# A convolution block in float32: splitting four of six Winograd products by column parity for seven blocks, with wide squares and a new planned order

## The chip, the cores and the metric

The kernel runs on one core of a Trainium2 chip. The core has a tensor engine (PE, with its weight loads shown apart as PEld), a vector engine (DVE), a scalar engine (ACT), a general engine (POOL) and a queue for transfers (SP). The metric is the device time of one execution in microseconds. Before the change it is 1743.63 us, the median of three runs (1743.13 to 1743.80).

## The reference, cut to what matters

The input x is 4 images of 128 channels by 128 by 128 pixels, all float32. Two layers follow each other, and each adds its result to its input.

```python
# layer 0
x = x + _L0_conv_ref(_gn(x), ...)     # twice the same block: on x and on x transposed, summed
# in the block, t = tokens x channels
t = _ln(t); y1 = _ln(t); t = t + silu(y1) @ W_out.T
y2 = _ln(t); wht = y2 @ W_whiten.T
k = square(relu(wht @ W_key.T)); kv = k @ W_value.T; r = sigmoid(wht @ W_recep.T)
t = t + r * kv
# layer 1
x = x + _L1_conv_ref(_gn(x), ...)     # 3x3 convolution of expert 0, bias, channel gate from the mean
```

`_gn` is a group norm over 32 groups of four channels, with statistics over a whole image. So layer 0 of an image can start only when all of its input has been read once, and layer 1 only when layer 0 of the whole image is done.

## The kernel before, in words

**Layer 0.** An image is 32 chunks of 512 pixels (`CH`), worked in 16 pairs; `layer0(g)` records the work of pair g (0 to 63 over the four images). A chunk is normalised (`st`, `rs`, `nb`, `t`), multiplied with the attention weights (`att`, line 954), normalised again and turned to channels, and then goes through four key products (`pk`, line 1033), a rectifier (`h`, line 1038), a square (line 1044 on ACT, line 1050 on DVE), four value products (`kv`, line 1071), one gate product (`pr`, line 1058), the gating `r` (line 1080, DVE) and the addition to x (line 1086, POOL). Line 1094 takes the statistics for the second group norm.

**Layer 1.** `conv(k, at)` records one block of 16 rows, eight per image, k from 0 to 31. It is a Winograd form along the rows: DVE makes six transforms `v0` to `v5` from the loaded rows `xc` (lines 1179 to 1193), six products `m0` to `m5` follow, and ACT and DVE combine them to four output rows (lines 1218 to 1239). A product is three matmuls on one PSUM bank, for the centre, left and right tap of a row (lines 1203 to 1205); the filters `uw` are reloaded per image and scaled (line 621), and four of them get a unit tap (line 627). `conv_setup(b, ...)` (lines 538 to 642) turns the image's statistics into the group norm and the gate: an aggregate (line 552), group means (`cpm`, 555), variances (`cpv`, 565), two small squeeze products (`cp`, 579, and `cpr`, 589), a tanh, and the scaled filters.

**Order.** No engine is programmed in the order of the text. Every operation is recorded with its engine, a cost and a priority (`op`), and `Plan.order` lists them once when the program is built: the earliest operation that can start wins, ties and near ties go by priority plus the number that `SHIFT` has for its name, and `ROOM` limits how many buffers of a kind are in use. So the convolution of image b is laid between the operations of layer 0 of image b+1, and that of the last image stands alone at the end. `FIRST_FILL` and the loop at the end of the kernel put filler products (`busy`, line 411) on PE where it has nothing else to do early in the run.

**What stands around the change.** Of the third image, blocks 17 to 23 are the last seven. In the trace, their products start at 1369, 1419, 1469, 1514, 1550, 1575 and 1593 us; the last value product of the fourth image starts at 1577.75 us. `SQUARES` says for each of the eight squares of a pair where it is done: the first row up to pair 16, the second from pair 17 (`SQUARES_AT`).

Of the kernel before, what the change touches and what calls it, by code (L numbers as in the profile page):

```python
# [23 lines left out]
    "R": -94.694, "Rc": 15.085, "Rm": -2.646, "S": 24.009, "T": -84.8, "Tz": -36.19, "W": -22.14,  # L24
    "ab": 37.315, "att": 1.644, "b": 31.731, "bn0": 11.794, "bn1": -17.35, "bn2": -15.592,
    "bx": 49.609, "c": 7.82, "cag": 6.719, "cav": -18.068, "cd": -103.804, "cp": -37.768,
    "cp1": -27.368, "cpm": -17.233, "cpr": -71.755, "cpv": -65.194, "cre": 48.407, "crt": -73.005,
    "csg": -26.086, "csp": -39.311, "cth": -29.247, "cve": 53.942, "e": 12.136, "e0": 14.7,
    "e1": -70.81, "e2": -55.971, "edge": 60.492, "fw": 14.887, "g": -16.106, "gag": -13.379,
    "gnb": -14.148, "gpm": -2.701, "gpv": -23.531, "grt": -1.635, "gsp": -6.989, "gve": -30.013,  # L30
    "hot": -13.329, "in": 26.361, "in0": 105.375, "kv": 3.816, "late": 12.753, "m0": 23.5,
    "m1": -101.213, "o": -54.585, "pk": 3.497, "pq": -18.954, "pr": 3.288, "q": -106.007,
    "raw": -61.508, "rc": -6.337, "re": -93.796, "silu": -97.676, "sq": -115.033, "sqd": -34.912,
    "t": -2.49, "tD": -49.255, "tR": 16.588, "tW": -20.948, "th": -60.823, "tt": 105.266,
    "u": 16.271, "us": -19.465, "ut": 67.807, "ut2": 9.337, "uw": -50.513, "v": 57.985, "w": 117.982,
    "w0": 44.736, "w1": -43.048, "w2": -6.943, "x": 70.181, "x1": -70.076, "xc": 6.78, "xd": 2.407,
    "xf": -58.371, "xo": -10.863, "xs": -54.606, "y": 24.867, "z": 15.121, "zD": 21.243,
    "zR": 18.813, "zW": -13.966,
}
SQUARES = (("DDAA", "DDAA"), ("AAAA", "AAAA"))  # L40
TAIL_BANKS = ("Bkv", "Btr", "Btr", "Bh", "Bconv", "Bh")
TAIL_HOMES = ("xc", "xc", "x", "x", "x", "xc", "xc", "x")
CONV_AT, CONV_STEP = 2.0, 2.0
LOOK = {'PE': 0.018, 'DVE': 0.087, 'ACT': 0.048, 'POOL': 0.004, 'SP': 0.048}
HASTE = 31.975
SQUARES_AT = 17
ROOM = dict(
    x=3, xd=2, xs=2, ut=3, t=7, z=2, y=2, zd=2, zc=2, td=2, tt=2, R=2, y2=2, h=6, r=2, xc=2, vt=3, v=4,
# [3 lines left out]
BACKLOG = 1.96  # L52
FIRST_U_ON_DVE = (2, 3)


XF_BUS, FIRST_XD, LATE_AT = 3.4, -25, -5
FILL_UNTIL, FILL_STEP = 330, 1.2
FIRST_FILL = {6: 3, 7: 2}
# [26 lines left out]
def S_ON(g):  # L85
    return "POOL" if T_BY_DMA(g) else "DVE"

# [155 lines left out]
def conv_preact_kernel(  # L243
# [42 lines left out]
        z=[P, SUB, C], y=[P, CH], y2=[P, CH], h=[P, CH], r=[P, CH],  # L286
        xc=[P, BLK_ROWS + 2, W], vt=[P, Q, W], v=[P, Q, W], yt=[P, Q, W], uw=[P, 3, P],
# [17 lines left out]
    def staged(name, n, src=None):  # L305
        t = sb.tile([P, n], F32, tag="h", name=name, bufs=ROOM["h"])
        if src is not None:
            nc.scalar.dma_start(t, src)
        return t
# [112 lines left out]
    READ, WRITE = (0, 0.85), (0, 0.4)  # L422

    def op(name, eng, cost, prio, emit, reads=(), writes=(), new=(), port=False, bus=0.0):
        return plan.op(name, eng, cost, prio + SHIFT.get(name, 0.0), emit, reads, writes, new, port, bus)
# [112 lines left out]
    def conv_setup(b, at):  # L538
# [90 lines left out]
        for i in (1, 2, 3, 4, 0, 5):  # L629
            t = ("uw", b, i)  # L630
            if b > 0:

                def fetch(i=i, t=t):
                    nc.sync.dma_start(make(t, "uw"), raw_u[i])

                op("uw", D, READ, at - 1, fetch, [(("raw", i), 0), (("ready", b - 1), 0)], [(t, 0)], [(t, "uw")], bus=0.65)
            op(
                "us", V, (0.52, 0.61), at, lambda i=i: scaled(i), [(c, 0), (t, 0)],
                [(t, 0), *([(("ready", b), 0)] if i == 5 else ())], (), True,
            )  # L640
            if i in TAP:
                op("ut2", V, (0.21, 0.29), at, lambda i=i: tapped(i), [(t, 0)], [(t, 0)], (), True)

# [92 lines left out]
    def layer0(g):  # L736
# [3 lines left out]
        if p * PAIR % PER == 0:  # L740
# [6 lines left out]
            for q in range(SUB):  # L747

                on_dve = k == 0 and q in FIRST_U_ON_DVE

                def lay(q=q, on_dve=on_dve):
                    rs, nb = gn0[b]
                    scale, bias = rs[:, q : q + 1], nb[:, q : q + 1]
                    if on_dve:
                        nc.vector.tensor_scalar(T[xd][:, q], T[xd][:, q], scale, bias, ALU.mult, ALU.add)
                    else:
                        nc.scalar.activation(T[xd][:, q], T[xd][:, q], AF.Identity, bias=bias, scale=scale)

                op(
                    "u", V if on_dve else A, (0.61, 0.7) if on_dve else (0.705, 0.82), g, lay, [(("gn0", b), 0), *((xd, a) for a in range(SUB))],  # L760
                    [(xd, ("u", q))],
                )
# [117 lines left out]
        for h in range(PAIR):  # L880
            r = (p * PAIR + h) % PER

            def turn(h=h, r=r):
# [5 lines left out]
                "ut", V, (0.61, 0.7), g, turn, [(xd, ("u", q)) for q in range(SUB)],  # L889
# [105 lines left out]
        for h in range(PAIR):  # L995
# [33 lines left out]
            for j in range(NH):  # L1029
                pk, hh = ("pk", g, h, j), ("h", g, h, j)  # L1030
# [6 lines left out]
                def relu(pk=pk, hh=hh, j=j):  # L1037
                    nc.scalar.activation(make(hh, "h"), T[pk], AF.Relu, bias=kbias[:, j : j + 1])  # L1038

                op("re", A, (0.572, 0.69), g, relu, [(pk, 0)], [(hh, 0)], [(hh, "h")])  # L1040
                if square_on(g, h, j) == "A":

                    def square(hh=hh):
                        nc.scalar.activation(T[hh], T[hh], AF.Square)  # L1044

                    op("sq", A, (0.52, 0.63), g, square, [(hh, 0)], [(hh, 0)])
                else:

                    def square(pk=pk, hh=hh, j=j):
                        nc.vector.scalar_tensor_tensor(  # L1050
                            T[hh], T[pk], kbias[:, j : j + 1], T[hh], ALU.add, ALU.mult
                        )

                    op("sqd", V, (0.605, 0.685), g, square, [(hh, 0), (pk, 0)], [(hh, 0)])
# [11 lines left out]
            for j in range(NH):  # L1066

                def value(j=j, kv=kv, h=h):
                    if j == 0:
                        make(kv, "Bkv")  # L1070
                    nc.tensor.matmul(T[kv], wv[:, j, :], T["h", g, h, j], start=(j == 0), stop=(j == NH - 1))  # L1071
# [3 lines left out]
                    [(("wv", "c"), 0), (("h", g, h, j), 0), *([(kv, j - 1)] if j else ())],  # L1075
# [32 lines left out]
    def conv(k, at):  # L1108
# [29 lines left out]

        def units(s):
# [8 lines left out]
        def put(n, tag):  # L1148
            if tag == "v" and ending:
                t = sb.tile([P, CH], F32, tag="h", name=n, bufs=ROOM["h"])  # L1150
                T[name_of(n)] = t.rearrange("p (q w) -> p q w", w=W)
                return T[name_of(n)]
            return make(name_of(n), tag)

        def do(name, eng, cost, fn, reads=(), writes=(), new=(), port=False):
            new = [(t, "h" if tag == "v" and ending else tag) for t, tag in new]
# [3 lines left out]
        TWO = (0.605, 0.685)  # L1160

        def inner(name, tag, fn, rows_in=(), tiles_in=(), extra=(), cost=TWO, inplace=False):
# [7 lines left out]
            else:  # L1170
                reads += [(("turned", k - 1, half), v) for v in HALVES[half]]
            do(
                "v" if tag == "v" else "pq", V, cost, fn, reads + ([(t, 0)] if inplace else []), writes,
                () if inplace else [(t, tag)], True,
# [3 lines left out]

        inner("p", "vt", lambda: stt(put("p", "vt"), rows(2), -4.0, rows(4), ALU.mult, ALU.add), (2, 4))
        inner("q", "vt", lambda: stt(put("q", "vt"), rows(1), -4.0, rows(3), ALU.mult, ALU.add), (1, 3))  # L1180
        inner(
            "v1", "v", lambda: stt(put("v1", "v"), get("p"), gn["mg6"], get("q"), ALU.add, ALU.add), (),  # L1182
            ("p", "q"), [(("gn1", b), 0)], (0.655, 0.73),
        )
        inner("v2", "v", lambda: tt(put("v2", "v"), get("p"), get("q"), ALU.subtract), (), ("p", "q"))
        inner("p2", "vt", lambda: tt(put("p2", "vt"), rows(4), rows(2), ALU.subtract), (2, 4))
        inner("q2", "vt", lambda: tt(put("q2", "vt"), rows(3), rows(1), ALU.subtract), (1, 3))
        inner("v3", "v", lambda: stt(put("v3", "v"), get("q2"), 2.0, get("p2"), ALU.mult, ALU.add), (), ("p2", "q2"))
        inner("v4", "v", lambda: stt(put("v4", "v"), get("q2"), -2.0, get("p2"), ALU.mult, ALU.add), (), ("p2", "q2"))
        inner("v0a", "v", lambda: tt(put("v0", "v"), rows(0), rows(2), ALU.subtract), (0, 2))  # L1190
        inner("v0b", "v", lambda: stt(get("v0"), get("v0"), 4.0, get("p2"), ALU.mult, ALU.add), (), ("p2",), inplace=True)
        inner("v5a", "v", lambda: tt(put("v5", "v"), rows(5), rows(3), ALU.subtract), (5, 3))
        inner("v5b", "v", lambda: stt(get("v5"), get("q2"), -4.0, get("v5"), ALU.mult, ALU.add), (), ("q2",), inplace=True)

        def product(i):
            tag = TAIL_BANKS[i] if ending else "Bconv"
            m, v = name_of(f"m{i}"), name_of(f"v{i}")

# [9 lines left out]

        def t0(n):
            return (name_of(n), 0)  # L1210

        def outer(name, fn, reads, writes, new=(), port=False):
# [5 lines left out]
            lambda: nc.scalar.activation(put("e1", "yt"), get("m1"), AF.Identity, bias=gn["beta"]),  # L1218
            [t0("m1"), (("gn1", b), 0)], [t0("e1")], [(name_of("e1"), "yt")],
        )  # L1220
        product(2)
# [4 lines left out]
            "e", A, (0.572, 0.69), lambda: nc.scalar.copy(put("e3", "yt"), get("m3")), [t0("m3")],  # L1226
            [t0("e3")], [(name_of("e3"), "yt")],
        )
        product(4)
# [91 lines left out]
```

## Time and profile before

| | |
|---|---|
| median of the runs | 1743.63 us |
| profiled execution | 1742.63 us |
| its span, first to last instruction | 1740.9 us |
| mean granted clock of PE | 0.997 of full |
| PE, DVE, ACT, POOL busy | 97%, 82%, 74%, 68% |
| HBM traffic over the span | 203 GB/s |
| key and value products on PE | 480.9 and 525.8 us busy |
| the three lines of the convolution products on PE | 197.7, 195.4 and 194.9 us busy |

A group line of the profile reads: line, engine, operation, tile written and tiles read, shape, count, then busy time in all and the mean of one in ns, then the idle time of that engine just before, and what ended it. A timeline line reads: start and length in us, engine, line, operation, tiles, shape, number of instructions merged, and in brackets the idle time before. A float32 matmul stands in the trace as two records. The ends of matmuls are modelled, so the pace of PE is read from starts.

### The profile page before, as it was taken

How to read it: one execution, taken by the hardware profiler on the slowest of the kernel's cores; microseconds unless marked ns; L12 is line 12 of the kernel's file. 1: busy time of each engine (PE TensorE's matmuls, PEld its weight loads, DVE VectorE, ACT ScalarE, POOL GpSimd, SP SyncE). 2: the span in 40 equal slices, each digit the busy share in tenths (PEclk: the TensorE clock that was granted, in tenths of full speed). 3: DMA queues.
4: the chain of work that ended last, by engine and by line, in shares of the span. 5: the costliest groups of instructions: out<-in, count | busy, mean ns of one | idle time of the engine just before them, and what ended most of it. 6: DMA issues, size and time to landing. Idle time of an engine off the chain costs nothing.

```text
span 1740.9 us, 18709 instructions
## 1 busy us (share of the span) xinstructions
PE 1690.7 (97%) x4872; PEld 815.7 (47%) x4872; DVE 1424.9 (82%) x2619; ACT 1293.8 (74%) x2656; POOL 1184.0 (68%) x1085
## 2 busy tenths in 40 slices
PE   5899999999999999999999999999999999999999
PEld 2444544444444445444445445454544444444443
DVE  5898888788889967798998887888897766448986
ACT  1999998898988887889889877998887875440000
POOL 1778887788987885879777886988878773310000
PEclk9999999999999999999999999999999999999999
DMA  9366675466577777578778877577776565215321
GB/s 326 91 213 202 193 219 194 145 206 230 153 250 246 252 230 236 199 232 247 250 245 245 254 238 240 178 218 236 241 254 199 183 204 176 101 75 224 154 98 73
DMA packets 140170, 354.66 MB, mean 204 GB/s; under 512 B 19079, under 2 KB 78750, under 8 KB 122782
## 3 DMA queue, kind: packets, MB, share of 16 engines
q1 hardware_dynamic: 139472, 352.99, 63.1%
q8 instruction: 39, 0.64, 0.2%
q14 instruction: 69, 0.57, 0.1%
q10 hardware_dynamic: 590, 0.46, 0.1%
HBM read 230.31 MB, written 123.07 MB: 203 GB/s over the span
## 4 chain that ended last, share of the span: by engine, by line
PE 71%; ACT 10%; POOL 8%; DVE 7%; DMA 2%; issue 2%; SPq 0%; ACTq 0%; DVEq 0%; POOLq 0%
PE kv L1071 19%; PE pk L1033 18%; PE m L1203 7%; PE m L1204 7%; PE m L1205 7%; PE att L954 5%; PE pr L1058 5%; ACT t L839 2%; ACT h L1038 2%; POOL rs L820 2%; ACT z L839 2%; DVE st L770 1%; ACT h L1044 1%; POOL x L1026 1%; POOL t L908 1%
## 5 line engine op out<-in xcount | busy, mean ns | idle before, releaser
L1071 PE MATMUL kv<-h,wv 128*128 128x512 f32 x1024 | 525.8, 598 | 4.6 <-DVE r L1080 2.6
L1033 PE MATMUL pk<-y,wk_s 128*128 128x512 f32 x1024 | 480.9, 595 | 4.7 <-ACT h L1038 3.1
L1038 ACT ACTIVATE h<-pk,kbias 128x512 f32<-128x512 f32 x512 | 336.1, 682 | 90.9 <-PE pk L1033 88.3
L1033 PEld LDWEIGHTS pk<-y,wk_s 128*128 128x128 f32 x1024 | 190.0, 190 | 239.3 <-issue 178.1
L1071 PEld LDWEIGHTS kv<-h,wv 128*128 128x128 f32 x1024 | 183.0, 190 | 205.3 <-issue 164.1
L1044 ACT ACTIVATE h<-h 128x512 f32<-128x512 f32 x444 | 267.5, 629 | 2.6
L1086 POOL TENSOR_TENSOR x<-x,r 128x512 f32<-128x512 f32 x128 | 169.8, 1327 | 132.0 <-DVE r L1080 128.5
L820 POOL TENSOR_TENSOR rs<-rs,nhalf 128x8 f32<-128x8 f32 (+1 forms) x134 | 227.2, 1700 | 47.3 <-ACT rs L817 45.1
L839 ACT ACTIVATE z<-t,nb,rs 128x128 f32<-128x128 f32 x512 | 208.7, 489 | 21.8 <-POOL nb L825 20.9
L839 ACT ACTIVATE t<-ut,nb,rs 128x128 f32<-128x128 f32 x512 | 209.7, 488 | 8.5 <-POOL nb L825 4.8
L908 POOL TENSOR_TENSOR t<-t,g 128x512 f32<-128x512 f32 x124 | 161.2, 1301 | 68.0 <-ACT t L839 67.6
L770 DVE BATCH_NORM_STATS2 st<-t 128x6 f32<-128x256 f32 x512 | 187.1, 410 | 22.9 <-POOL t L911 22.7
L1203 PE MATMUL m<-v,uw 128*128 128x512 f32 x384 | 197.7, 596 | 3.9 <-DVE v L1182 3.9
L1204 PE MATMUL m<-v,uw 128*128 128x508 f32 x384 | 195.4, 590 | 0.0
L1205 PE MATMUL m<-v,uw 128*128 128x508 f32 x384 | 194.9, 589 | 0.0
L1015 POOL TENSOR_TENSOR y<-tt,R 128x512 f32<-128x512 f32 x96 | 130.9, 1367 | 59.8 <-PE pk L1033 46.9
L1026 POOL TENSOR_TENSOR x<-tt,x 128x512 f32<-128x512 f32 x124 | 162.5, 1324 | 3.9 <-DMA tt<-ts 3.7
L911 POOL TENSOR_TENSOR t<-t,b 128x512 f32<-128x512 f32 x124 | 162.7, 1319 | 2.6
L954 PEld LDWEIGHTS att<-wo,y 128*128 128x128 f32 x1024 | 130.9, 192 | 51.7 <-issue 33.1
L1063 ACT ACTIVATE r<-pr,rbias 128x512 f32<-128x512 f32 x128 | 87.1, 681 | 72.6 <-PE pr L1058 36.2
L1058 PE MATMUL pr<-y,wr_s 128*128 128x512 f32 x256 | 132.3, 600 | 3.9 <-ACT h L1038 3.0
L954 PE MATMUL att<-wo,y 128*128 128x128 f32 x1024 | 132.8, 276 | 0.4 <-ACT y L947 0.3
(160 smaller groups left out, 2278.6 us busy)
## 6 DMA issues: line engine op xcount, KB each, us to landing
xd<-in_x SPq DMA_DIRECT2D x128, 256.0 KB
x<-in_x SPq DMA_DIRECT2D x32, 1024.0 KB
xo<-x SPq DMA_DIRECT2D x32, 1024.0 KB
R<-rd SPq DMA_DIRECT2D x63, 512.0 KB
ts<-td SPq DMA_DIRECT2D x248, 128.0 KB
tt<-ts SPq DMA_DIRECT2D x62, 512.0 KB
out<-xc SPq DMA_DIRECT2D x31, 1024.0 KB
xc<-xo SPq DMA_DIRECT2D x24, 1152.0 KB
```

The lines of the kernel that those rows point to most:

```text
L770: nc.vector.bn_stats(st[:, i : i + 2, :].rearrange("p n f -> p (n f)"), two)
L820: nc.gpsimd.tensor_tensor(T[rs][:, part], T[rs][:, part], nhalf[:, :k], ALU.pow)
L839: nc.scalar.activation(dst[:, s, :], src[:, s, :], AF.Identity, bias=nb[:, i : i + 1], scale=rs[:, i : i + 1])
L954: nc.tensor.matmul(pa[:, ts(m, P)], T[y][:, ts(m, P)], wo2, start=True, stop=True)
L1033: nc.tensor.matmul(make(pk, "Bh"), wk_s[:, ts(j, P)], T[y2], start=True, stop=True)
L1038: nc.scalar.activation(make(hh, "h"), T[pk], AF.Relu, bias=kbias[:, j : j + 1])
L1044: nc.scalar.activation(T[hh], T[hh], AF.Square)
L1058: nc.tensor.matmul(make(pr, "Bh"), wr_s, T[y2], start=True, stop=True)
L1071: nc.tensor.matmul(T[kv], wv[:, j, :], T["h", g, h, j], start=(j == 0), stop=(j == NH - 1))
L1203: nc.tensor.matmul(pc, u[:, 1], vv, start=True, stop=False)
L1204: nc.tensor.matmul(pc[:, :, 1:W], u[:, 0], vv[:, :, 0 : W - 1], start=False, stop=False)
L1205: nc.tensor.matmul(pc[:, :, 0 : W - 1], u[:, 2], vv[:, :, 1:W], start=False, stop=True)
```

## The change

Five things are done together.

- For blocks 17 to 23 (`PARITY`) products 0, 1, 3 and 5 are split by the parity of the pixel's column. The transform v is laid down with the even columns in one half of the tile and the odd ones in the other. With filter taps u0, u1, u2, an even output needs u1 of the even column, u0 of the odd one before and u2 of the odd one beside it; and u1 of even plus u2 of odd is u1 of (even + odd) plus (u2 - u1) of odd. So one matmul of u1 with the sum of the halves (`su`, `cm`) serves both parities, and each parity has two matmuls of its own, with the differences of the filters (`ud`). The shared product is added by DVE (`cs`). Each of these matmuls has 256 columns or 252.
- Squares of two neighbours are done by ACT as one instruction of 1024 elements (`W`); the rectified tiles become double tiles (`h`, three instead of six). Up to pair 16 three instead of four squares of a pair stay on DVE.
- `FIRST_FILL` loses an entry: two instead of five early filler products on raw input.
- `zd` and `td` go from two buffers to one; the transforms of the last image take `t` tiles instead of `h` tiles.
- All the numbers of the planner (`SHIFT`, `LOOK`, `HASTE`, `BACKLOG`, `XF_BUS`) are new, so the order of the whole program is.

```diff
-SQUARES = (("DDAA", "DDAA"), ("AAAA", "AAAA"))
+SQUARES = (("DAWW", "DDWW"), ("WWWW", "WWWW"))
+SUM_BANK = "Btr"
-LOOK = {'PE': 0.018, 'DVE': 0.087, 'ACT': 0.048, 'POOL': 0.004, 'SP': 0.048}
-HASTE = 31.975
+LOOK = {'PE': 0, 'DVE': 0.079, 'ACT': 0.059, 'POOL': 0.002, 'SP': 0.194}
+HASTE = 63.69
 ROOM = dict(
-    x=3, xd=2, xs=2, ut=3, t=7, z=2, y=2, zd=2, zc=2, td=2, tt=2, R=2, y2=2, h=6, ...
+    s=2, ud=4,
+    x=3, xd=2, xs=2, ut=3, t=7, z=2, y=2, zd=1, zc=2, td=1, tt=2, R=2, y2=2, h=3, ...
-FIRST_FILL = {6: 3, 7: 2}
+FIRST_FILL = {7: 2}
+def PARITY(k):
+    return (0, 1, 3, 5) if 17 <= k < 24 else ()
...
+                    nc.vector.tensor_tensor(make(ud, "ud"), u[:, 0::2], u[:, 1:2].to_broadcast([P, 2, P]), ALU.subtract)
+                op("ud", V, (0.335, 0.42), at, beside, [(t, 0)], [(ud, 0)], [(ud, "ud")], True)
...
+                elif how == "W" and not first:
+                    def square(hh=hh):
+                        x = T[hh].rearrange("p a b -> p (a b)")
+                        nc.scalar.activation(x, x, AF.Square)
...
+            if tag == "v" and int(n[1]) in halves:
+                whole = T[name_of(n)].rearrange("p q w -> p (q w)")
+                T[name_of(n)] = whole.rearrange("p (e q k) -> p q k e", e=2, q=Q)
...
+                def both(i=i, su=su):
+                    x = flat_halves(i)
+                    dst = make(su, "s").rearrange("p (q k) -> p q k", q=Q)
+                    nc.vector.tensor_tensor(dst, x[:, 0], x[:, 1], ALU.add)
...
+                def parts():
+                    bank = make(m, tag)
+                    pc = bank.rearrange("p (e q k) -> p e q k", e=2, q=Q)
+                    T[m] = bank.rearrange("p (e q k) -> p q k e", e=2, q=Q)
+                    u, d, x = T["uw", b, i], T[ud], flat_halves(i)
+                    nc.tensor.matmul(pc[:, 0], d[:, 1], x[:, 1], start=True, stop=False)
+                    nc.tensor.matmul(pc[:, 0, :, 1:], u[:, 0], x[:, 1, :, : W // 2 - 1], start=False, stop=True)
+                    nc.tensor.matmul(pc[:, 1], d[:, 0], x[:, 0], start=True, stop=False)
+                    nc.tensor.matmul(pc[:, 1, :, : W // 2 - 1], u[:, 2], x[:, 0, :, 1:], start=False, stop=True)
+
+                def shared():
+                    nc.tensor.matmul(make(mm, SUM_BANK)[:, : CH // 2], T["uw", b, i][:, 1], T[su], start=True, stop=True)
...
+            def add():
+                t = by_parity(get(n))
+                row = T[name_of(f"mm{i}")][:, : CH // 2].rearrange("p (q k o) -> p q k o", q=Q, o=1)
+                tt(t, row.to_broadcast([P, Q, W // 2, 2]), t, ALU.add)
```

## The prediction

> **What bounds the kernel now.** I read the busy shares of the page first, then the table by stages, then the timeline of the tensor engine (PE) at the three places where it is not full.
>
> ```profile
> span 1740.9 us, 18709 instructions
> PE 1690.7 (97%) x4872; PEld 815.7 (47%) x4872; DVE 1424.9 (82%) x2619; ACT 1293.8 (74%) x2656; POOL 1184.0 (68%) x1085
> ...
> 300.00:400.00 100.00, 94.76 (x309) 47.79 (x308) 82.56 (x162) 89.64 (x186) 80.42 (x76) 0.98 0.56 177
> 1200.00:1300.00 100.00, 99.85 (x277) 47.53 (x276) 90.98 (x159) 85.44 (x177) 87.03 (x75) 1.00 0.77 240
> 1300.00:1400.00 100.00, 100.00 (x275) 47.24 (x274) 77.47 (x143) 78.58 (x162) 78.86 (x69) 1.00 0.58 192
> 1400.00:1500.00 100.00, 100.00 (x281) 47.87 (x280) 64.79 (x107) 61.95 (x118) 50.65 (x41) 1.00 0.52 170
> 1500.00:1600.00 100.00, 99.53 (x251) 45.06 (x250) 60.56 (x107) 35.77 (x63) 18.49 (x15) 1.00 0.37 141
> ```
>
> In the stage rows the columns after the length are PE, weight loads, DVE, ACT, POOL. From 1200 to 1600, where the convolution of the third image runs beside layer 0 of the fourth, PE is full and DVE is idle for 9.0+22.5+35.2+39.4 = 106 us. There PE work is time. Busy is no proof of pace, so I take starts:
>
> ```profile
> 1500.16 1.95 PE L954 MATMUL att<-wo,y 128*128 128x128 f32 x16
> 1501.95 1.02 PE L1071 MATMUL kv<-h,wv 128*128 128x512 f32 x2
> 1502.81 5.31 PE L1033 MATMUL pk<-y,wk_s 128*128 128x512 f32 x12
> 1507.96 0.59 PE L1071 MATMUL kv<-h,wv 128*128 128x512 f32 x1
> ```
>
> Twelve 512-column records take 1507.96-1502.81 = 5.15 us, 429 ns each; sixteen 128-column ones 1.79 us, 112 ns each. A float32 product is two records.
>
> The places where PE is not full: the start, about 300 to 330, and the close, between the last value product of the fourth image and its first convolution product.
>
> ```profile
> 29.49 7.20 PE L411 MATMUL fill<-xf,gmat 128*128 128x512 f32 x10
> 36.53 0.95 PE L498 MATMUL pm<-mv,gturn 128*128 128x1 f32 x8
> ...
> 31.04 1.02 DVE L493 BATCH_NORM_AGGREGATE mv<-st 128x2 f32<-128x192 f32 x1
> 37.74 0.17 DVE L509 COPY mg<-pm 128x5 f32<-128x5 f32 x1 [5.67 <-PE pm L500]
> ...
> 303.05 1.05 PE L498 MATMUL pm<-mv,gturn 128*128 128x1 f32 x8 [1.73 <-ACT h L1038]
> ...
> 1577.75 1.02 PE L1071 MATMUL kv<-h,wv 128*128 128x512 f32 x2
> 1578.61 1.02 PE L1203 MATMUL m<-v,uw 128*128 128x512 f32 x2
> 1581.17 1.02 PE L1203 MATMUL m<-v,uw 128*128 128x512 f32 x2
> ...
> 1612.37 2.07 PE L1203 MATMUL m<-v,uw 128*128 128x512 f32 x2 [3.42 <-DVE v L1182]
> ```
>
> The statistics of the first image are whole at 32.06, but the group means stand behind filler products until 36.53. One convolution product (three matmuls) costs 1581.17-1578.61 = 2.56 us. From the last value product's end (1578.61) to the first product of the fourth image's convolution 33.8 us pass; eleven products (28.2 us) cover most of it, and 3.42 us stay idle. The last 48 products and the last store take 1740.9-1612.4 = 128.5 us.
>
> **The change part by part.** *Split products.* Each of 28 products becomes four matmuls over half the columns and one shared one. A 256-column record, on the line between the two rows above, is 112+(429-112)/3 = 218 ns, a 252-column one 214 ns. Product: (3x218+2x214)x2 = 2.16 us against 2.56; 28x0.40 = **11.2 us less PE work**. Bounds: 11.8 if it is half of 429 exactly, 0 if weight loads surface (rival). The weight loads of the 128-column rows hide at 112 ns a pair, so I keep 11.2.
>
> The Trainium skill ("TensorE: Matmul & The Clock Gate", LDWEIGHTS, and Part 3, The mechanism) says that a load takes its columns over 1.2 GHz, about 107 ns, and that loads run beside matmuls in flight only when they use other rows of the array. With ten records a product instead of six that would be an estimated 0.43 us more and would eat the whole saving. The 112 ns pairs above, each with its load, speak against it here.
>
> *Vector work for it.* 28 sums of halves (256 elements; nearest row, the 256-element statistics, 410 ns, issued every 0.33), 28 additions of the shared product (nearest row, the 512-element additions from PSUM, 681 ns, issued every 0.60), 4 differences of filters (0.4): 9.2+16.8+1.6 = 28 us of DVE, in a stage with 106 us idle. Hidden, price 0. Ops that write or read the halves interleaved keep 0.60 by the row of the statistics, which hop 512 bytes between neighbours and take 410 ns for 256 elements against 674 for 512 contiguous ones; the far end is 1.2 us, about 12 ops x 7 blocks x 0.6 = 50 us more. 28+50 = 78 is still under 106; only the close would feel it (below). The skill ("SBUF — State Buffer", the note on cachelines in Door 1) warns that each step past a 16-byte line costs; by it the far end would hold, and the statistics row does not show such a cost for reads. No row shows it for writes.
>
> *Squares.* 444 narrow squares on ACT (629 ns, issued every 0.52) and 68 on DVE become 17, 222 wide ones and 51. A wide one lies between 0.52 (nothing for width) and 1.04 (twice); I take 0.95. ACT -11 us, DVE -10 us over the run; neither bounds. A wide square makes the first value product of a pair wait for the second activation, about 0.6 us, while PE takes other chunks' products; without that cover 256 pairs x 0.6. h has three double tiles for six single ones, the same bytes. Price 0, from -3 to +3.
>
> *Rooms.* zd and td drop to one buffer: a pair's two transposes on DVE (and all behind them) now wait for the four stores of the pair before on SP's queue, not of two before. Pairs are about 25 us apart (the value products of pairs 48 and 52 start at 1181.4 and 1278.7), a store is 128 KB. Price 0; without cover a few us each. POOL keeps its work; SP gets no new transfer, but the places of many move.
>
> *Fewer early products.* Five fillers on raw input become two. They start at 29.45 at half clock (0.85 a record), four records end at 32.9: the means start right behind the statistics, not at 36.5. But the clock that became full at 34.9 will not have by then: the earlier small products show 1.71/8 = 0.21 us a record at half clock against 0.11, so means and variances lose 2 us of the 3.6. **-1.8**, between -3.6 and 0 (the 15 fillers that follow run cold and push the first transposition).
>
> *New order.* Everything is planned again. The built order has the second image's means at 10.9 pairs of value products instead of 11.4, so half a pair (10 us) more work behind them to cover the change of images. Idle there: 1.73 and 0.94 us before products, smaller ones, and 3.4 us at clock 0.5 from 304.5, some 7 us. I take **-2.5**; bounds 0 and -7. Elsewhere PE waits little and I take 0.
>
> *The close.* In the new order only two ordinary, three split and two shared products follow the last value product: 2x2.56+3x1.73+2x0.43 = 11.2 us instead of 28.2. So PE does 28.2-11.2-11.2 = **5.8 us more before** that point, which then stands at 1578.6+5.8-1.8-2.5 = 1580.1. After it, by the rows of before and the new order: means product behind shared, ordinary, shared, split (5.2), variances behind an ordinary one (8.0), squeeze product behind split, shared, split (12.2); rectify 1.0 (1591.95 to 1592.98), second product 0.4, tanh 0.7, the first vectors of the new block and the row 1.9: 16.2. Then six scalings 0.57 each, an output sum, four taps, the border and the first transform, 6.0: **22.2 us**, against 33.8. PE idles 10 us of it, and as in before (clock 0.5 for 3.4 us from 1611.8) restarts cold: 0 to 1.7 more than before, 0.5 taken. Bounds for the close: 18 (no queue on DVE) and 36.8, when nothing overlaps: 12.4 PE + 19.8 DVE (the 44 instructions that the new order has there, at their spacing in before) + 4.6 of round trips. It is nearest to the low end since DVE's queue there loses most of two blocks.
>
> **Sum.** First product of the fourth image at 1580.1+22.2 = 1602.3, 10.1 earlier; +0.5 cold: -9.6 us. The profiled execution took 1742.63 (span 1740.9 and 1.7 around it), 1.0 under the median of 1743.63. 1742.63-9.6 = 1733.0, and on the median's scale **1734.0**.
>
> **Rivals.**
> - *More comes in:* close at 18, change of images -7, start -3.6: 1734.0-4.2-4.5-1.8 = **1723.5**. For it: a whole new order; against: each at its bound.
> - *Interleaved vectors cost double and the early gains fail:* in the close seven such ops add 4.2; start and change of images give nothing (+4.3): **1742.5**, no change.
> - *Weight loads surface:* nothing saved on PE; the last value product comes 28.2-12.9-4.3 = 11.0 later than before, close 23.5: 1613.1, with 0.5 cold 1.2 later: **1744.8**. Against it: the 112 ns pairs.
> - *Slower, the close serialises:* DVE is in order, and block 23's sums stand between the setup steps, each behind a PE product. At 36.8 the first product comes at 1616.9, 4.5 late, +0.5: **1748.6**. The gain is gone from 31.8 us on, and it is slower by 0.2% from 35.3 on. For it: before took 33.8; against it: in before DVE had two blocks to finish there.
>
> **How the numbers follow.** About 0.2% (3.5 us) is what a measurement of this kernel can tell from no change. Forecast 0.54, more 0.21, no change 0.10, loads 0.07, slower 0.08. Faster: the first two and a little of the third, 0.76; same: the rest of the third and half of the loads' case, with the noise of both, 0.14; slower 0.10. The range takes in most of the first rival and reaches to the second: 1726 to 1743. The forecast's own range is 1729 to 1739.
>
> **What would show it.** Records of 256 columns about 218 ns apart; means at 33 us, not 36.5; PE still full from 1200 on, with DVE some 28 us busier; the last value product near 1580 and the first product of block 24 some 22 us after it, behind about 10 us of idle PE and a cold clock. Wrong would be: starts of the split records near 270 ns, DVE full beside an idle PE before 1580, or a close above 32 us.

## The result, and the profile after

The changed kernel takes 1750.80 us (median of 20 runs, 1743.03 to 1757.16); the kernel before, run beside it, takes 1742.85 (1739.00 to 1748.51). The ratio is 1.0045, with a 95% interval of 1.0034 to 1.0057: **slower by 0.45%, 8 us**, where 9.6 us less were forecast. The profiled execution of the changed kernel took 1748.30 us, 2.5 under its median.

The busy shares of its page, and the shares of the engines in the chain of work that ended last:

```profile
span 1746.6 us, 18860 instructions
PE 1679.6 (96%) x4978; PEld 834.5 (48%) x4978; DVE 1439.8 (82%) x2662; ACT 1282.7 (73%) x2451; POOL 1190.5 (68%) x1085
...
PE 53%; POOL 17%; DVE 12%; ACT 8%; DMA 5%; issue 3%; SPq 1%; ACTq 0%; DVEq 0%; POOLq 0%
```

The same stage rows as before (after the length: PE, weight loads, DVE, ACT, POOL, then the granted clock):

```profile
300.00:400.00 100.00, 98.84 (x320) 49.00 (x319) 78.60 (x158) 96.96 (x191) 82.85 (x80) 1.00 0.58 191
1200.00:1300.00 100.00, 98.48 (x283) 47.45 (x282) 86.23 (x167) 83.90 (x163) 82.00 (x73) 1.00 0.73 235
1300.00:1400.00 100.00, 97.80 (x303) 52.83 (x302) 80.24 (x134) 63.05 (x109) 60.65 (x49) 1.00 0.53 176
1400.00:1500.00 100.00, 96.74 (x317) 54.04 (x316) 81.10 (x130) 66.00 (x114) 57.28 (x49) 1.00 0.52 171
1500.00:1600.00 100.00, 99.05 (x288) 52.97 (x286) 67.54 (x105) 46.92 (x64) 28.85 (x21) 1.00 0.32 112
```

PE is busy for 11 us less, and the span is 5.7 us longer. From 1200 to 1500, where PE stood at 99.85 to 100, it is now at 96.7 to 98.5. DVE between 1300 and 1600 went from 202.8 to 228.9 us. In the chain PE's share is 53%, where it was 71%, and POOL (17% after 8%) and DVE (12% after 7%) have most of what PE lost: the chain runs through waits more often.

The PE timeline at the three places that the prediction spoke of: the start, a split product, the close.

```profile
29.67 3.76 PE L422 MATMUL fill<-xf,gmat 128*128 128x512 f32 x4
33.22 1.71 PE L511 MATMUL pm<-mv,gturn 128*128 128x1 f32 x8
...
1593.91 1.02 PE L1116 MATMUL kv<-h,wv 128*128 128x512 f32 x2
...
1597.33 0.59 PE L1302 MATMUL mm<-s,uw 128*128 128x256 f32 x2
1597.76 0.59 PE L1296 MATMUL m<-v,ud 128*128 128x256 f32 x2
1598.19 0.59 PE L1297 MATMUL m<-v,uw 128*128 128x252 f32 x2
...
1608.93 0.48 PE L602 MATMUL cpr<-s,a 16*128 16x128 f32 x2 [1.62 <-DVE a L596]
...
1617.16 2.07 PE L1312 MATMUL m<-v,uw 128*128 128x512 f32 x2 [7.63 <-DVE v L1253]
```

The means start at 33.22 (36.53 before). Two 256-column records take 0.43 us, 215 ns each (216 in the median of the stage). The last value product starts at 1593.91 and ends about 1594.8; block 24 starts 22.4 us later. All this is as forecast. But the last value product was to stand near 1580, and it stands 16 us later than before: part of that is convolution work moved ahead of it, and the rest is waits. The following rows of waits on PE between 1300 and 1600 (engine, what waited, for what: us in all, times, longest) name the longest:

```profile
PE kv L1116 <- DVE r L1125: 1.8, 2, 1.3
PE mm L1302 <- DVE e L1325: 1.7, 1, 1.7
PE mm L1302 <- DVE s L1281: 1.3, 2, 0.9
```

The idle time of PE can be summed from the starts of its matmuls: what a start-to-start distance has over its columns/1.2 + 2.7 ns (429 ns for 512 columns, by the rows of before) is idle or a cold clock. By pairs of layer 0:

| idle and cold, us | before | after | after's order, whole products |
|---|---|---|---|
| to pair 3 | 42.0 | 41.0 | 42.4 |
| pairs 4 to 15 | 17.4 | 14.8 | 14.9 |
| pairs 16 to 47 | 16.4 | 24.2 | 25.7 |
| pairs 48 to 63 | 4.5 | 13.9 | 6.8 |
| close | 6.6 | 13.1 | 11.0 |

PE's own work fell by 11.7 us through the split and 2.6 through three fewer fillers; idle rose by 20.1. Two places gave it back: pairs 16 to 47, where no product is split, and pairs 48 to 63, where they are. (The 6.5 us more in the close stood in the forecast, as some 10 us of idle PE there.) Each column is one execution; the second and third took 2.5 us less and 3.0 us more than their medians, so a few us between these two columns mean little. The rise in pairs 16 to 47 is no accident of one execution: in four more traces of the new order (whole products with two buffers, plain transforms, and both kernels without sums) it is 7 to 11 us.

### The profile page after: what moved, and what is told of

The parts are those of the page before. It is cut to its first block, busy times and chain, and to the rows that moved or that the text cites. A ratio compares the mean times of both kernels' runs of the same rounds, so it can differ in the third digit from the quotient of the medians.

```text
span 1746.6 us, 18860 instructions
## 1 busy us (share of the span) xinstructions
PE 1679.6 (96%) x4978; PEld 834.5 (48%) x4978; DVE 1439.8 (82%) x2662; ACT 1282.7 (73%) x2451; POOL 1190.5 (68%) x1085
## 4 chain that ended last, share of the span: by engine, by line
PE 53%; POOL 17%; DVE 12%; ACT 8%; DMA 5%; issue 3%; SPq 1%; ACTq 0%; DVEq 0%; POOLq 0%
PE kv L1116 14%; PE pk L1058 13%; PE m L1312 5%; PE m L1313 5%; PE m L1314 5%; POOL rs L845 4%; PE pr L1103 4%; PE att L979 3%; DMA xs<-in_x 2%; POOL t L933 2%; POOL x L1131 2%; POOL t L936 2%; POOL four L816 2%; ACT t L864 2%; ACT z L864 2%
## 5 line engine op out<-in xcount | busy, mean ns | idle before, releaser
L1058 PE MATMUL pk<-y,wk_s 128*128 128x512 f32 x1024 | 494.6, 596 | 9.0 <-ACT h L1064 3.4
L1064 ACT ACTIVATE h<-pk,kbias 128x512 f32<-128x512 f32 x512 | 340.3, 680 | 111.7 <-PE pk L1058 72.9
L845 POOL TENSOR_TENSOR rs<-rs,nhalf 128x8 f32<-128x8 f32 (+1 forms) x134 | 234.2, 1753 | 38.3 <-ACT rs L842 38.2
L1083 ACT ACTIVATE h<-h 128x1024 f32<-128x1024 f32 x222 | 234.1, 1055 | 2.2
L1312 PE MATMUL m<-v,uw 128*128 128x512 f32 x328 | 169.1, 597 | 10.1 <-DVE v L1253 8.8
L1313 PE MATMUL m<-v,uw 128*128 128x508 f32 x328 | 167.3, 592 | 0.0
L1314 PE MATMUL m<-v,uw 128*128 128x508 f32 x328 | 166.9, 591 | 0.0
L816 POOL TENSOR_TENSOR four<-four,nhalf 128x8 f32<-128x8 f32 x63 | 110.5, 1756 | 21.4 <-ACT four L812 21.3
```

Source lines behind the costliest of these rows:

```text
L845: nc.gpsimd.tensor_tensor(T[rs][:, part], T[rs][:, part], nhalf[:, :k], ALU.pow)
L1058: nc.tensor.matmul(make(pk, "Bh"), wk_s[:, ts(j, P)], T[y2], start=True, stop=True)
L1064: nc.scalar.activation(dst[:, j % 2], T[pk], AF.Relu, bias=kbias[:, j : j + 1])
L1083: nc.scalar.activation(x, x, AF.Square)
L1312: nc.tensor.matmul(pc, u[:, 1], vv, start=True, stop=False)
L1313: nc.tensor.matmul(pc[:, :, 1:W], u[:, 0], vv[:, :, 0 : W - 1], start=False, stop=False)
```

## The experiments

Times are medians; each ratio is against the kernel before on the same chip. To change one part and not the order, most kernels record the whole program twice: one variant is planned, and the other is emitted in that written order.

**1. Undo the split in the new order.**

```diff
-    return (0, 1, 3, 5) if 17 <= k < 24 else ()
+    return ()      # emitted in the order planned with (0, 1, 3, 5)
```

> The written order, buffers and squares are those of the changed kernel, instruction for instruction; only the split is undone: the 28 products are whole again, and the 28 sums of halves, 28 shared products, 28 additions and 4 filter differences are gone. Theory A (the order is what costs): the time of PE comes back, 28 x 0.42 = 11.7 us, less some 4 us of idle that PE had before shared products (3.8 us in the trace of the changed kernel), so 1756 to 1760, slower than the changed kernel by 6 to 9. Theory B (the split's own vector work is what costs, because it delays the gating and the transforms on DVE): the 9.4 us of idle that pairs 48 to 63 had more than before and half of the 5.7 us more in the close go as well, so 1746 to 1750, no slower than the changed kernel.

1750.53 us, 1.0032 (1.0020 to 1.0045). The time of the changed kernel, though PE has the 11.7 us of work again; the last column of the table shows that 7.1 us of idle in pairs 48 to 63 go with the split. As it is written, the split gives nothing measurable in this order, and the order itself, with its squares and rooms, is slower than before.

**2. The split alone, in the old order.** The sums, differences, shared products and additions are set directly behind the operations that they belong to. With `zd` and `td` at one buffer (31 DVE operations had to stand back for that):

```diff
+    order = inserted(order_of_before)
-    zd=2, td=2
+    zd=1, td=1, s=3, ud=4
```

> The written order of the kernel before, with the split put into it: each sum of halves right behind its transform, each shared product right behind its own product, each addition right ahead of its reader, each filter difference behind its filter; zd and td have one buffer so that the new tiles fit, and some 30 instructions of DVE stand a little later for that. Theory A: PE loses 11.7 us of work and little idle comes, except in the close, where 7 of the 11 covering products get shorter (3 us) while the chain under them keeps its length or grows by the added vector work (2 us): 1733 to 1738. Theory B: the idle of the changed kernel's pairs 48 to 63 (9.4 us more) and of its close (6 us more) comes here too: 1743 to 1748.

1804.28 us, 1.0324 (1.0302 to 1.0346). To take the buffers out of it, the same with two buffers, the sums and differences in the tiles of the row loads (nothing stands back; in this kernel and its variant with fewer fillers part of the third image's convolution is not computed as in the reference, while the instructions and their sizes are the same):

> The old written order with the split put into it as in old_order_split, but zd and td keep their two buffers: the sums of halves and the filter differences lie in the two input tiles (xs) that nobody uses any more while the fourth image is worked. ACT, POOL and SP run the very order of the kernel before, and no instruction of DVE or PE stands back. Theory A (the split pays in an order with two buffers): PE loses 11.7 us of work, the close keeps its length: 1733 to 1739. Theory B (the split's vector work is given back as waits wherever it is put; in the changed kernel's order 7.2 us of idle in pairs 52 to 63 went with it and 2 in the close): 1741 to 1747. If it is near 1800 like old_order_split, the split itself made those 60 us and not the buffers.

1776.31 us, 1.0181 (1.0166 to 1.0197), still 33 us slower than before. The profiled execution of this kernel took 3996.67 us and is no guide; the trace of the variant with fewer fillers (experiment 4) says why. One of its stages, and the waits on its PE from 1380 to 1600:

```profile
1400.00:1500.00 100.00, 90.55 (x272) 49.24 (x271) 70.24 (x113) 61.21 (x117) 49.60 (x41) 0.91 0.54 171
```

```profile
PE kv L1099 <- DVE r L1108: 11.9, 5, 3.5
PE att L982 <- DVE t L987: 2.9, 2, 2.2
```

DVE is busy for 70 of 100 us there, and PE waits for it. The gating `r`, which reads the PSUM bank of the value products and so frees it for the next, stands in DVE's queue behind other work, the new transforms, sums and additions among it. The granted clock of the stage is 0.91; it is 0.72 from 1400 to 1410 and 0.66 from 1460 to 1470, where waits of 3.1 and 3.5 us for `r` lie, and 1.00 from 1420 to 1430.

That is not all of the loss. Against the old order with fewer fillers and whole products, the last value product ends 20.9 us later (1594.48 against 1573.63), and from there to the first product of block 24 it takes 47.7 us instead of 33.8. So 14 us are lost in the close: PE waits 4.4 us for the aggregate of the statistics there, and 3.1 and 3.5 us for other work of DVE. The transforms are interleaved here as in the changed kernel (experiment 6); the split with plain transforms was not run in the old order.

**3. One buffer, two buffers.** `zd` and `td` at one buffer in the old order, whole products; and at two in the new order, whole products, where `st` went from 6 tiles to 4 and `rs` from 6 to 3.

> The kernel before, its written order, whole products; only zd and td have one buffer instead of two (a handful of DVE's transposes stand a little later, as they must). If the single buffers made the 60 us of old_order_split: 1785 to 1805, with idle already in pairs 32 to 47, ahead of any split block. If the split made them: 1743 to 1750.

> The changed kernel's written order with whole products, as in after_order_whole, and with two buffers for zd and td. If the single buffers cause the 8 us of idle that its pairs 16 to 47 have more than before: 1741 to 1745. If the order itself does: 1749 to 1752, no change from after_order_whole.

1773.28 us, 1.0174 (1.0155 to 1.0194), and 1750.20, 1.0040 (1.0022 to 1.0057). In an order planned for two buffers the second one is worth 30 us. The new order was planned for one, and a second gives it nothing, though the fewer `st` and `rs` tiles could have hidden a small gain. The row of the transposes into `zd` in the changed kernel points the same way: over the whole run DVE stands idle ahead of them for 6.8 us, and of that 0.8 for a store.

```profile
L875 DVE STREAM_TRANSPOSE zd<-z 128x512 f32<-128x512 f32 x84 | 58.0, 695 | 6.8 <-ACT z L864 5.9 <-DMA zs<-zd 0.8
```

So the rooms are hardly the 8 us of pairs 16 to 47.

**4. Fillers.** Two of five early fillers in the old order, and none; and the first together with the split of experiment 2.

```diff
-                    busy(times,
+                    busy(times if k == 7 else 0,
```

> The kernel before with two early fillers on raw input instead of five and nothing else moved. If the means then start right behind the statistics and the shift goes through to the end: 1.5 to 3.5 us faster, 1739 to 1741.5. If PE's clock is then late and takes it back, or a later wait (a load, the change of images) absorbs it: no change, 1742 to 1744.

> The kernel before with none of its five early filler products on raw input instead of two of five; the order is otherwise the same. If fillers only stand ahead of the means: 1 to 3 us less than with two, 1736 to 1739. If the two left keep the clock up for the first small products: as with two or slower, 1739 to 1744.

> The two above together, in the old written order. Theory A: the two add up, 1730 to 1736, which beats both kernels. Theory B: 1741 to 1747.

> The same with two early fillers on raw input instead of five, which alone gave 4.8 us. Theory A: 1729 to 1734, which beats both kernels. Theory B: 1736 to 1743.

Two: 1739.37 us, 0.9970 (0.9959 to 0.9981). None: 1740.07, 0.9982 (0.9970 to 0.9995). With the splits 1796.57 (7.7 less than without) and 1774.07 (2.2 less). **The kernel before with two early fillers is faster than both kernels**, by 0.3% and 0.75%.

**5. The split's vector work.** The new order without the 28 sums and 28 additions of the shared product; and with the sums on POOL.

```diff
-                do("su", V, (0.335, 0.42), both, ...)
-            do("cs", V, TWO, add, ...)
-                    nc.tensor.matmul(..., T["uw", b, i][:, 1], T[su], ...)
+                    nc.tensor.matmul(..., T["uw", b, i][:, 1], flat_halves(i)[:, 0], ...)
```

```diff
-                    nc.vector.tensor_tensor(dst, x[:, 0], x[:, 1], ALU.add)
+                    nc.gpsimd.tensor_tensor(dst, x[:, 0], x[:, 1], ALU.add)
```

> The changed kernel in its own written order, but without the 28 sums of halves and the 28 additions of the shared product: they are left out, and the shared matmul reads the even half instead of the sum. The products on PE stay as they are. So part of the third image's convolution is not computed. Theory A (the split's vector work queues ahead of what PE waits for, and its waits pay back what PE saves): the waits of pairs 52 to 63 fall from 10.1 to about 3 us and the close by 1 to 3, 1741 to 1745 us. Theory B (only the new order costs, the split is free and worth little because its matmuls overlap worse than forecast): within 2 us of the changed kernel, 1749 to 1753.

> The changed kernel in its own written order, the 28 sums of halves done by POOL at the places where DVE did them; the additions of the shared product stay on DVE. DVE loses 28 instructions of about 550 ns, 15 us, in a stage where POOL is busy for 18 to 80%. If the place in DVE's queue is the cost: part of the 6.9 us comes back, 1744 to 1749. If a sum on POOL is later than on DVE (slower, and behind the additions to x) and the shared product waits for it: 1751 to 1757.

Without them, so that part of the third image's convolution is left out, 1743.94 us, 1.0007 (0.9996 to 1.0017): 6.9 less. With the sums on POOL 1754.55, 1.0062 (1.0045 to 1.0079): no gain. The new wait there, of 6.3 us:

```profile
PE mm L1305 <- POOL s L1284: 6.3, 7, 2.1
```

A sum takes 0.72 us or more on POOL (0.41 on DVE) and stands behind POOL's other work, and the shared product waits for it.

**6. The interleaved writes.** The trace of the changed kernel held one more suspect. The groups of DVE from 1300 to 1620 (busy us, mean ns):

```profile
L1251 DVE TENSOR_TENSOR v<-xc 128x512 f32<-128x512 f32 x15 | 17.7, 1180 | 0.7 <-PE m L1299 0.7
L1253 DVE SCALAR_TENSOR_TENSOR v<-q,p 128x512 f32<-128x512 f32 x15 | 16.1, 1097 | 8.4 <-PE m L1299 8.3
L1281 DVE TENSOR_TENSOR s<-v 128x256 f32<-128x256 f32 x28 | 15.3, 553 | 0.4
L1253 DVE SCALAR_TENSOR_TENSOR v<-q,v 128x512 f32<-128x512 f32 x7 | 9.3, 1332 | 0.0
L1253 DVE SCALAR_TENSOR_TENSOR v<-p,mg,q 128x512 f32<-128x512 f32 x8 | 8.6, 1080 | 2.5 <-PE m L1299 2.5
L1253 DVE SCALAR_TENSOR_TENSOR v<-v,p 128x512 f32<-128x512 f32 x8 | 8.2, 1025 | 0.0
```

Sorted by what they write, with no two-operand work on POOL beside them, transforms that lay even and odd columns into two halves take 1.04 to 1.14 us, the others 0.68 (0.74 with the scalar `mg`). So the layout was turned round: transforms in pixel order, and the sums and matmuls read every second element. Once with the sums, once without sums and additions.

```diff
-                T[name_of(n)] = whole.rearrange("p (e q k) -> p q k e", e=2, q=Q)
+                T[name_of(n)] = whole.rearrange("p (q k e) -> p q k e", e=2, q=Q)
```

> The changed kernel, but the transforms of the split products are laid down in pixel order; the sums on DVE and the matmuls on PE read the even and odd columns with a step of two elements. Nothing else changes. If the interleaved writes cost 0.38 us each, 42 of them 16 us of the vector engine, and reads with a step of two cost nothing on PE or DVE: the transforms fall to 0.68 us and the time by 3 to 6 us, 1744 to 1748. If the reads with a step of two cost as much as the writes did: 256-column records start more than 216 ns apart or the sums take over 0.41 us, and the time is 1750 to 1760.

> The same without the 28 sums and the 28 additions of the shared product, which are left out, the shared matmul reading the even columns instead of the sum. If vector work is all that stood against the 11.7 us that the split saves on PE: 1738 to 1741 us, 10 to 12 below the changed order with whole products. If the interleaved writes are hidden: as the run without sums, 1742 to 1746.

1744.75 us, 1.0004 (0.9991 to 1.0018), **6.0 us below the changed kernel** and 7.1 by the ratios; without sums 1744.73, 1.0002 (0.9988 to 1.0017), which is no less. So the 7 us are the price of neither part alone. Without the interleaved writes the sums and additions cost nothing that can be measured (1.0004 against 1.0002), and without the sums and additions the interleaved writes cost nothing either (1.0007 in experiment 5 against 1.0002). Only both together cost 7 us, and taking out either brings them back. The same groups with plain transforms:

```profile
L1281 DVE TENSOR_TENSOR s<-v 128x256 f32<-128x256 f32 x28 | 14.8, 534 | 0.3
L1253 DVE SCALAR_TENSOR_TENSOR v<-q,p 128x512 f32<-128x512 f32 x15 | 12.4, 838 | 8.8 <-PE m L1299 8.8
L1251 DVE TENSOR_TENSOR v<-xc 128x512 f32<-128x512 f32 x15 | 12.0, 802 | 1.3 <-PE m L1299 1.3
L1253 DVE SCALAR_TENSOR_TENSOR v<-q,v 128x512 f32<-128x512 f32 x7 | 6.0, 853 | 0.0
L1253 DVE SCALAR_TENSOR_TENSOR v<-p,mg,q 128x512 f32<-128x512 f32 x8 | 5.9, 737 | 2.6 <-PE m L1299 2.6
L1253 DVE SCALAR_TENSOR_TENSOR v<-v,p 128x512 f32<-128x512 f32 x8 | 5.5, 682 | 0.0
```

The five groups of transforms take 41.8 us here and 59.9 in the changed kernel, 18 us less of DVE. The sums keep their time with reads of step two. The two traced executions took the same time (1748.37 us here, 1748.30 for the changed kernel), so they show less of the gain than the medians. This one has a granted clock of 0.993 against 0.997 and is 4.7 us late at the first value product of pair 48, ahead of any split product; from there to the last value product it takes 389.9 us against 393.5. DVE runs its 2662 instructions in the same order in both. How a longer queue reaches PE is seen at one place. In the changed kernel, DVE and then PE:

```profile
1463.33 1.53 DVE L1281 TENSOR_TENSOR s<-v 128x256 f32<-128x256 f32 x1
1464.78 0.68 DVE L984 TENSOR_TENSOR t<-att,t 128x512 f32<-128x512 f32 x1
1465.38 1.06 DVE L1253 SCALAR_TENSOR_TENSOR v<-v,p 128x512 f32<-128x512 f32 x1
...
1466.95 0.39 DVE L1281 TENSOR_TENSOR s<-v 128x256 f32<-128x256 f32 x1
1467.27 0.67 DVE L1125 SCALAR_TENSOR_TENSOR r<-r,kv 128x512 f32<-128x512 f32 x1
...
1467.99 1.12 PE L1116 MATMUL kv<-h,wv 128*128 128x512 f32 x2 [1.33 <-DVE r L1125]
```

The same place with plain transforms, on DVE:

```profile
1465.46 0.68 DVE L1253 SCALAR_TENSOR_TENSOR v<-v,p 128x512 f32<-128x512 f32 x1
...
1466.72 0.82 DVE L1281 TENSOR_TENSOR s<-v 128x256 f32<-128x256 f32 x1
1468.35 0.69 DVE L1125 SCALAR_TENSOR_TENSOR r<-r,kv 128x512 f32<-128x512 f32 x1 [0.80 <-PE kv L1116]
```

In the first, `r` comes behind a queue that never stops, and PE idles 1.33 us for it. In the second DVE has caught up and itself waits 0.80 us for PE. The first sum was held at this place in both (1.53 us, and 1.36 with plain transforms; the last section says by what). The transforms make the difference: 1.06 us against 0.68 for the one shown, and 2.10 against 0.68 for another just ahead, which ran beside an operation on POOL.

**7. Squares.** Each wide square as two narrow ones, each directly behind its rectifier, in the new order.

> The changed kernel in its own written order, each wide square done as two narrow ones, each directly behind its own rectifier. 222 instructions of 1055 ns become 444 of about 630 (issued every 0.52). If the wide squares make the first value product of a pair wait, and this is the 7.8 us that PE idles more in pairs 16 to 47, the time falls to 1743 to 1747 us. If those waits are of the order (vector engine and rooms), it stays within 3 us of the changed kernel or is slower by the more work of ACT, 1749 to 1755.

1797.97 us, 1.0312 (1.0294 to 1.0331). ACT's squares take 279.8 instead of 234.1 us, and the time goes up by about as much, though ACT is busy for only 73% of the changed kernel. In an order laid out for wide squares they are worth 47 us. What they are worth against an order laid out for narrow ones was not measured, so their part in pairs 16 to 47 stays open.

**8. What an order alone is worth.** One number of the planner changed by a little, everything else the same: in the kernel before the nearness `LOOK` for DVE, PE or POOL set to the changed kernel's value, and in the changed kernel the one for DVE set back.

```diff
-LOOK = {'PE': 0.018, 'DVE': 0.087, 'ACT': 0.048, 'POOL': 0.004, 'SP': 0.048}
+LOOK = {'PE': 0.018, 'DVE': 0.079, 'ACT': 0.048, 'POOL': 0.004, 'SP': 0.048}
```

> The kernel before with one number of the planner changed: how near in time two operations of the vector engine must be for the priority to decide, 0.087 to 0.079, the value of the changed kernel. Every operation, tile and duration is the same; only the order is planned again. If an order alone, planned by other numbers, is worth some us: 1747 to 1760. If the planner's orders are all about as good, and the new order of the changed kernel lost for another reason: 1741 to 1746.

> The kernel before, planned again with another number: the nearness in time for PE 0.018 to 0, the value of the changed kernel. Operations, tiles and durations are the same. If any plan that was not selected by runs loses: 1750 to 1775. If the loss of the first such run was of its own number: 1740 to 1747.

> The kernel before, planned again with the nearness in time for POOL 0.004 to 0.002, the value of the changed kernel. As for the run before: 1750 to 1775 if any plan not selected loses, 1740 to 1747 if not.

> The changed kernel, planned again with one number set back: the nearness in time for DVE 0.079 to 0.087, the value of the kernel before. If its own order is one that was selected, as that of before: 1756 to 1785. If its order is an ordinary one, and that is why it lost against before: 1742 to 1756.

The kernel before: 1763.50 us (1.0112, 1.0094 to 1.0130), 1772.89 (1.0179, 1.0164 to 1.0193) and 1764.10 (1.0122, 1.0109 to 1.0135). The changed kernel: 1773.53 (1.0172, 1.0157 to 1.0187), 23 us above its own time. So both orders look picked: each of these four plans, next to one of them, loses 20 to 31 us with the same operations. In the first of them most of the loss between 1180 and 1300 is one wait:

```profile
PE m L1203 <- DVE v L1193: 9.8, 1, 9.8
```

## Why the prediction was wrong

Three steps failed: the vector work that was taken as hidden, the new order that was taken as free, and the part of the split's saving that arrives. The runs give each term a measured value, from differences of the ratios (each good to about 3 us):

| term | forecast | measured | from |
|---|---|---|---|
| fewer early products | -1.8 | -5.2 | experiment 4 |
| new order with its close, squares and rooms | +3.4 | +10.8 | 1 against 4 |
| split with plain transforms | -11.2 | -4.9 | 6 against 1 |
| interleaved writes, beside the sums | 0 | +7.1 | changed kernel against 6 |
| sum | -9.6 | +7.8 | result: +0.45% |

The forecast of the second row is the rest of its sum: change of images -2.5, 0.5 cold, and 5.4 from the close without the split. Two borders between rows are a choice. The 7.1 could as well stand as 6.9 at the sums and additions (experiment 5). And the first row was measured in the old order; with the 1.7 us that the changed kernel's own trace shows for it, the second row is +7.3.

- **"Ops that write or read the halves interleaved keep 0.60": failed.** Writes were priced by a row of reads, the statistics. They take 1.06 us against 0.68. The far end, 1.2 a piece, was near the truth per instruction; its 84 instructions were 42, 16 us of DVE. The Trainium skill ("SBUF — State Buffer", the note on cachelines in Door 1), which the prediction weighed and put aside, was right for these writes, which hop from half to half; it asks for two hits to a 16-byte line, which the step of two 4-byte elements in experiment 6 has.
- **"Hidden, price 0" by 106 us of idle DVE: failed, and it made the sign.** Sums (15.3 us busy), additions (18.9) and the longer writes (16) fit into the 106 us, as the prediction's own test asked, and together still cost 7 us; without either part the result would have been no change. DVE had idle time enough, but not where the work fell. The instructions on which PE's next work hangs stand in the same queue. In the old order 33 us were lost, part of them with 30% of DVE idle in the stage from 1400, and 14 in the close. Either part of the new work alone was indeed free in the new order (experiment 6).
- **"Elsewhere PE waits little and I take 0" for the new order: failed, by as much again.** Pairs 16 to 47, with no split product, idle 8 us more than before. A plan is not neutral: those next to before's lose 20 us and more. It was bounded from the change of images alone. That the idle went down there (17.4 to 14.8, clock 1.00 in the row from 300) was right. Which part of the 8 us is the wide squares' stays open (experiment 7).
- **Split products, 11.2 us of PE work: right on PE** (11.7; 215 ns against 218), but only 4.9 arrive with plain transforms. Reads with a step of two take 10 to 13 ns more a record, 2.6 us in all. Where the rest goes no run shows: without sums and with the halves apart, where these reads have no step, the time is the same (1743.94).
- **Fewer early products: right in the changed kernel's trace.** Fillers to the end of the variances: 29.49 to 39.38 before, 29.67 to 37.85 after, 1.7 us less, and the small products run at half pace as forecast. In the old order they ran near full pace (eight records in 1.16 us), and the gain was 3.3 in the trace and 5.2 in the times (3.3 to 7.1 by the interval), where the bound was 3.6.
- **Rooms, price 0: right here** (1750.20 against 1750.53), in an order that was planned with them; the old order, planned with two buffers, lost 30 us with one. The few us that the prediction named for no cover were too few.
- **The close: right**, 22.4 us against 22.2, with 10.8 us of PE idle. It was not luck: the means product comes 4.9 us after the last value product (5.2 forecast), the variances 8.2 (8.0), the squeeze product 12.3 (12.2).
- **The rivals.** Weight loads did not surface: 215 ns. The slower rival, a close that serialises, did not come in the new order, but its reason, sums of block 23 in DVE's queue between the setup steps, fits the old order, where the close with the split took 47.7 us (experiment 2). The rival that named double cost for interleaved vectors had half of the cause, but put it in the close (4.2 us) instead of the whole stage, and its end, 1742.5, was no change.

## What to carry to other kernels

Idle time of an engine that takes its queue in order covers new work only if nothing that the bounding engine waits for stands behind that work; look at the queue around each insertion, not at the stage's sum. When a kernel's order was chosen among many plans, a new plan is a change of its own with a price, here 7 to 31 us and always a loss, and it must be measured apart from the edit. Undo each part of a change alone and both together: here two removals gave 7 us each, and both no more than one. Price a write by a row of writes, and where one side of a transfer must hop, try letting the reader step rather than the writer.

## What the runs showed of the hardware

- A 512-element float32 write on DVE that alternates between two places 1 KB apart took 1.04 to 1.14 us, a contiguous one 0.68. Reads from PSUM in the same alternation cost nothing: the output additions, which read the banks of split products 0 and 5 that way in seven of eight cases, took no longer than the one that does not. Nor did reads with a step of two (a sum 0.417 us against 0.411, medians of those that nothing held). On PE such reads took 226 instead of 216 ns per 256 columns.

```profile
L1366 DVE TENSOR_TENSOR xc<-m,e 128x512 f32<-128x512 f32 x8 | 5.4, 675 | 0.0
L1363 DVE TENSOR_TENSOR xc<-m,c 128x512 f32<-128x512 f32 x8 | 5.4, 672 | 0.0
```

- Some sums were long for another reason. Of the changed kernel's 28, 23 took 0.39 to 0.43 us and five 0.76 to 1.53. These five are just those that began while a 512-element operation of two tensors ran on POOL, and each ended 0.28 us after that operation did; four that began before such an operation, and four beside 8-element operations of POOL, were not held. One of them, and the product that it held up in the end, on the timeline of the changed kernel:

```profile
1388.77 1.26 POOL L933 TENSOR_TENSOR t<-t,g 128x512 f32<-128x512 f32 x1
...
1388.83 1.49 DVE L1281 TENSOR_TENSOR s<-v 128x256 f32<-128x256 f32 x1
...
1390.91 0.67 DVE L1325 TENSOR_TENSOR e<-mm,e 128x512 f32<-128x512 f32 x1
...
1391.63 0.70 PE L1302 MATMUL mm<-s,uw 128*128 128x256 f32 x2 [1.71 <-DVE e L1325]
```

  The addition of the shared product, two places behind that sum on DVE, frees the bank for the next shared product, and PE's wait for it is the longest between 1300 and 1600. The Trainium skill ("GPSIMD Engine Reference", 1. Specifications) lists the SBUF interfaces as shared by the two engines, with contention when DVE has two SBUF inputs, as the sums have. The trace fits that; no run tested it.
